# Four deals per tile, from one DMA queue or from two: the first layer of a graph network on one core

## The chip, the cores and the metric

The kernel runs on one core of a Trainium2 chip. The metric is the device time of one execution in microseconds (us); lower is better. Before the change it is 2586.3 us, the median of 3 runs (2586.27 to 2588.68).

## The reference

Four graph layers on x (2708 nodes x 512) with one adjacency matrix (2708 x 2708, zeros and ones, symmetric), all in f32. After each layer the result is added to x and layer-normalised. The change sits in layer 0:

```python
# layer 0: masked attention with 8 heads of 64
adj  = max(adj, eye)
q, k, v = x @ Wq[h], x @ Wk[h], x @ Wv[h]
att  = softmax(q @ k.T / 8 - 1e16 * (1 - adj))
out  = sum_h (att @ v) @ Wo[h]
x    = layernorm(x + out)
# layer 1: normalised adjacency times a two-step linear map
# layer 2: additive attention over the graph, leaky slope 0.2
# layer 3: normalised adjacency times x, linear map, relu
```

## The kernel before, in words

Layer 0 first projects x into KT (keys, transposed), V (values) and queries, which go to memory as `qtd` (lines 281 to 371; GpSimd issues those stores at line 348). Then it works through 84 full **pairs** and one last one: 21 chunks of 128 query rows (c) times 4 pairs of heads (p), and one remaining chunk of 20 rows.

For each pair the stages are these (class Pair, lines 399 to 528):

- `scores` (lines 426 to 448): TensorE multiplies queries by keys (line 417) into PSUM tiles of two heads; VectorE adds the mask, stores the scores in s and keeps their maxima (line 439). The 2708 columns are cut in two halves (k = 0 and 1) of 1408 and 1300, and each half in three parts.
- `maxima` (line 452), on VectorE, and `weights` (line 458), on ScalarE: exp of the scores, in place.
- The weights must then be turned, so that key nodes lie on the partitions. For the first 8 of the 128-column chunks of each half (16 of 22 chunks) this is done without TensorE: `blocks` (lines 460 to 467) transposes 32 x 32 blocks within the partitions on VectorE into a tile d (128 partitions x 2048 f32, 1 MB), and `deal` (lines 469 to 477) moves them across partitions by DMA into a tile e. d has four **node groups** of 32 partitions (g = 0 to 3); group g goes to `e[:, g]`, 32 source partitions with four runs of 2 KB each onto 128 destination partitions: 256 KB in one DMA, four DMAs for each tile, in the order g = 0, 2, 1, 3.
- `turn` (line 490) transposes the other 6 chunks on TensorE, and ScalarE copies them out of PSUM.
- `values` (lines 517 to 523): 44 products of V with the turned weights accumulate into av (line 509); ScalarE copies av to ot (line 527) and GpSimd issues the store of ot to `otd` in memory (line 528, 64 KB).

Tiles and buffers that matter: d has 2 buffers (line 385) and e has 3 (line 386). A pair uses one d and one e for each half. So a `blocks` may write its d only when the four deals out of the previous tile in this buffer have landed, and a deal may write its e only when TensorE has read the weights that lay there.

The order on TensorE, VectorE and ScalarE is written out by hand (manual_schedule, lines 609 to 651). One turn of that loop deals with three pairs: new (scores), cur (second half's blocks and deal, turn) and late (values). In each turn VectorE first writes the new pair's scores, then `cur.blocks(1)` (both heads, one instruction of 128 x 2048), then `new.blocks(0)` (one head at a time, two instructions of 128 x 1024), and the deals follow each:

```python
                if late is not None:
                    late.values()
                if cur is not None:
                    cur.blocks(1)
                    cur.deal(1)
                if new is not None:
                    for j in range(2):
                        new.blocks(0, slice(j, j + 1))
                    new.deal(0)
```

The queues of SyncE (SP) and GpSimd (POOL) are not under that manual schedule: the framework's scheduler places their instructions. On SP stand all eight deals of a turn and, once in four turns, the loads of the next chunk (queries, line 185, and three pieces of the adjacency rows, line 177). On POOL stands the store of ot, one for each pair. After layer 0 the other three layers follow with products, DMAs of adjacency tiles and small operations; the change does not touch them.

Of the kernel before, what the change touches and what calls it, by code (L numbers as in the profile page):

```python
# [22 lines left out]
def kernel(  # L23
# [22 lines left out]
    nc = tc.nc  # L46
# [99 lines left out]
    with ExitStack() as l0:  # L146
# [252 lines left out]
        class Pair:  # L399
# [69 lines left out]
            def deal(self, k):  # L469

                e = ep.tile([P, KD4, 2, DEALT, 32], F32, tag="e", name=f"e{self.c}_{self.p}_{k}")
                for g in (0, 2, 1, 3):
                    nc.sync.dma_start(
                        e[:, g].rearrange("p j m x -> p (j m x)"),
                        self.D[k][32 * g : 32 * g + 32].rearrange("p i j m x -> p i (j m x)"),
                    )
                self.E[bounds[k]] = e
# [908 lines left out]
```

## Time and profile before

| what | value |
|---|---|
| median of 3 runs | 2586.3 us |
| the profiled execution's own time | 2586.55 us |
| its span | 2584.8 us, so 1.75 us lie around it |
| mean granted TensorE clock | 0.989 |
| PE / DVE / ACT / POOL busy over the span | 97% / 76% / 45% / 12% |
| moved by SP's DMA queue (q1) | 392.0 MB, 53.4% of 16 engines' span |
| moved by POOL's DMA queue (q0) | 16.7 MB, 1.9% |
| pair loop of layer 0 | about 217 to 1228 us |
| DVE busy in 300 to 600, 600 to 900, 900 to 1200 us | 289.0, 291.5, 288.6 of 300 us each |
| ACT busy in the same | 224.7, 226.5, 223.1 of 300 us |
| DMA share in the same | 0.79, 0.79, 0.79 of 16 engines, 217 to 221 GB/s |

Rows of the profile name line, engine and operation, what is written and read, and how many; then busy time and mean duration, and the idle time that lay before them on their engine, with what ended most of it. The releaser after the arrow is inferred: of several waits it names the one that came last. SPq and POOLq are the queues of the DMA-issuing instructions: their durations are the time to issue, not to move the data. Durations of TensorE's matmuls are modelled, so a full PE is not by itself proof that PE is the limit.

### The profile page before, as it was taken

How to read it: one execution, taken by the hardware profiler on the slowest of the kernel's cores; microseconds unless marked ns; L12 is line 12 of the kernel's file. 1: busy time of each engine (PE TensorE's matmuls, PEld its weight loads, DVE VectorE, ACT ScalarE, POOL GpSimd, SP SyncE). 2: the span in 40 equal slices, each digit the busy share in tenths (PEclk: the TensorE clock that was granted, in tenths of full speed). 3: DMA queues.
4: the chain of work that ended last, by engine and by line, in shares of the span. 5: the costliest groups of instructions: out<-in, count | busy, mean ns of one | idle time of the engine just before them, and what ended most of it. 6: DMA issues, size and time to landing. Idle time of an engine off the chain costs nothing.

```text
span 2584.8 us, 42415 instructions
## 1 busy us (share of the span) xinstructions
PE 2514.1 (97%) x15551; PEld 1562.0 (60%) x15551; DVE 1959.6 (76%) x4541; ACT 1155.6 (45%) x2070; POOL 316.4 (12%) x322
## 2 busy tenths in 40 slices
PE   9999999999999999999899999899999999999997
PEld 4886777777777777776456444444444466444465
DVE  2669999999999999998474777888777874443544
ACT  2105777777777777776011001565665640000000
POOL 2210000000000000000210000243333430000000
PEclk9999999999999999999899999999999999999999
DMA  5115878778778787787753444344433213644633
GB/s 174 52 51 145 223 197 232 215 216 234 217 210 231 211 237 212 216 220 181 212 174 90 126 121 145 118 153 139 127 110 116 64 31 111 186 140 143 178 103 106
DMA packets 221498, 411.43 MB, mean 159 GB/s; under 512 B 28765, under 2 KB 48911, under 8 KB 221292
## 3 DMA queue, kind: packets, MB, share of 16 engines
q1 hardware_dynamic: 215052, 392.00, 53.4%
q0 software_dynamic: 6240, 16.73, 1.9%
q8 instruction: 123, 2.02, 0.3%
q14 instruction: 83, 0.68, 0.1%
HBM read 213.55 MB, written 16.72 MB: 89 GB/s over the span
## 4 chain that ended last, share of the span: by engine, by line
issue 49%; PE 40%; DVE 4%; POOL 3%; DMA 2%; ACT 1%; SPq 1%; POOLq 0%; ACTq 0%; DVEq 0%
PE acc L808 12%; PE acc L914 7%; PE m L1218 5%; PE pf L820 3%; PE psk L261 2%; POOL otd L528 2%; PE ph L900 1%; PE psq L261 1%; PE psv L261 1%; PE po L754 1%; PE p L945 1%; PE psv L357 1%; PE acc_t L808 1%; PE psq L309 1%; PE pz L820 1%
## 5 line engine op out<-in xcount | busy, mean ns | idle before, releaser
L458 ACT ACTIVATE s<-s,nm 128x1408 f32<-128x1408 f32 (+1 forms) x340 | 481.2, 1416 | 236.7 <-DVE nm L452 236.7
L439 DVE CUSTOM_DVE_ANT_0 s<-pss,adj 128x469 f32<-128x469 f32 (+2 forms) x1020 | 565.8, 622 | 1.1 <-PE pss L417 0.6
L417 PE MATMUL pss<-KT,qt 64*128 64x469 f32 (+2 forms) x2016 | 461.4, 559 | 7.0 <-DVE mx L439 4.8
L464 DVE STREAM_TRANSPOSE d<-s 128x1024 f32<-128x1024 f32 (+1 forms) x255 | 393.6, 1580 | 34.9 <-DMA e<-d 21.7
L417 PEld LDWEIGHTS pss<-KT,qt 64*128 64x128 f32 x2016 | 227.9, 186 | 200.0 <-issue 113.7
L808 PE MATMUL acc<-pt,x 128*128 128x512 f32 (+1 forms) x880 | 335.1, 540 | 12.7 <-ACT pt L861 9.7
L509 PE MATMUL av<-e,V 128*64 128x128 f32 x5376 | 308.8, 273 | 2.5 <-DMA e<-d 2.5
L509 PEld LDWEIGHTS av<-e,V 128*64 128x64 f32 x5376 | 296.8, 137 | 3.0 <-issue 3.0
L808 PEld LDWEIGHTS acc<-pt,x 128*128 128x128 f32 x880 | 158.8, 193 | 188.7 <-issue 164.4
L914 PE MATMUL acc<-at,h 128*128 128x512 f32 (+1 forms) x504 | 196.8, 543 | 0.0
L872 POOL TENSOR_TENSOR cs<-cs,pt 128x512 f32<-128x512 f32 (+2 forms) x110 | 157.4, 1431 | 203.2 <-ACT pt L861 200.1
L528 POOL DMA_DIRECT2D otd<-ot x84 | 45.4, 540 | 979.2 <-ACT ot L527 950.8
L859 DVE TENSOR_TENSOR pt<-pt,at 128x512 f32<-128x512 f32 (+2 forms) x132 | 107.4, 821 | 76.0 <-ACT pt L858 75.6
L1248 ACT ACTIVATE z<-pz,rdeg 128x512 f32<-128x512 f32 (+1 forms) x22 | 15.2, 689 | 310.4 <-PE pz L820 310.4
L94 ACT ACTIVATE ln_t<-lnve 128x1 f32<-128x1 f32 x88 | 17.7, 201 | 304.2 <-DVE lnve L108 304.0
L914 PEld LDWEIGHTS acc<-at,h 128*128 128x128 f32 x504 | 90.2, 190 | 101.4 <-issue 98.5
L490 PE MATMUL pst<-ident,s 128*128 128x128 f32 x1020 | 131.3, 279 | 0.0
L861 ACT ACTIVATE pt<-pt 128x512 f32<-128x512 f32 (+2 forms) x132 | 76.1, 579 | 109.4 <-DVE pt L860 109.2
L509 PEld LDWEIGHTS av<-pt,V 128*64 128x64 f32 x1680 | 90.0, 136 | 52.7 <-issue 52.5
L925 DVE SCALAR_TENSOR_TENSOR cs<-at,rdeg,cs 128x512 f32<-128x512 f32 (+2 forms) x126 | 86.2, 684 | 42.8 <-DMA at<-in_adjT_dram 41.8
L490 PEld LDWEIGHTS pst<-ident,s 128*128 128x128 f32 x1020 | 105.6, 134 | 17.3 <-issue 15.5
L509 PE MATMUL av<-pt,V 128*64 128x128 f32 x1680 | 110.3, 278 | 0.0
(348 smaller groups left out, 3484.5 us busy)
## 6 DMA issues: line engine op xcount, KB each, us to landing
e<-d SPq DMA_DIRECT2D x680, 256.0 KB
at<-in_adjT_dram SPq DMA_DIRECT2D x210, 256.0 KB
a<-in_adj_dram SPq DMA_DIRECT2D x38, 677.0 KB
adj<-in_adj_dram SPq DMA_DIRECT2D x42, 512.0 KB
at_a<-in_adjT_dram SPq DMA_DIRECT2D x40, 256.0 KB
at_c<-in_adjT_dram SPq DMA_DIRECT2D x40, 256.0 KB
at_f<-in_adjT_dram SPq DMA_DIRECT2D x40, 256.0 KB
adj<-in_adj_dram SPq DMA_DIRECT2D x21, 330.0 KB
```

The costliest lines, as they stand in the source:

```text
L261: nc.tensor.matmul(ps[:, p, :], ws[i][:, k, p * P : (p + 1) * P], xs[i][:, k, :], start=(k == 0), stop=(k == FC - 1),)
L417: nc.tensor.matmul(pss[j][:, :w], qt[h, self.p, :], KT[h, self.p, n0 : n0 + w], start=True, stop=True)
L439: nc.vector.tensor_tensor_reduce(out=s[:, j, h0:h1], in0=pss[j][:, : h1 - h0], in1=a[:, n0 + h0 : n0 + h1], scale=1.0, scalar=LOW, op0=ALU ...
L458: nc.scalar.activation(s, s, AF.Exp, bias=self.nm[:, j : j + 1], accum_out=self.sums(j, k))
L464: nc.vector.transpose(self.D[k].rearrange("p i j m x -> p j m i x")[:, heads], self.s[k][:, heads, : DEALT * P].rearrange("p j (m i x) -> ...
L490: nc.tensor.transpose(pt[:q, t, j, :], self.s[f][:, j, o : o + q], ident)
L509: nc.tensor.matmul(self.av[j * KD : (j + 1) * KD, out], V[:, m, h * KD : (h + 1) * KD], weights[j], start=(self.done == 0), stop=(self.don ...
L808: nc.tensor.matmul(acc[k][:, :w], last[0][g : g + mr, :] if m == NC - 1 else values[:mr, k * P : (k + 1) * P], moving[g : g + mr, :w], sta ...
L859: nc.vector.tensor_tensor(pt[:mr, :w], pt[:mr, :w], at[:mr, :w], ALU.subtract)
L872: nc.gpsimd.tensor_tensor(sums[:mr, :w], sums[:mr, :w], pt[:mr, :w], ALU.add)
L914: nc.tensor.matmul(acc[hc][:, :w], lastH[g : g + mr, :] if m == NC - 1 else H[m][:mr, hc * P : (hc + 1) * P], at[g : g + mr, :w], start=(m ...
L1218: nc.tensor.matmul(acc[k][:, : moving.shape[1]], combined[which, m][:, k * P : (k + 1) * P], moving, start=(m == 0), stop=(stop and m == N ...
```

## The change

In `deal`, the DMAs of node groups 2 and 3 are issued by GpSimd; those of groups 0 and 1 stay with SyncE. Size, shape, source and destination of every DMA are the same, and so is the order in which the code names them.

```diff
                 e = ep.tile([P, KD4, 2, DEALT, 32], F32, tag="e", name=f"e{self.c}_{self.p}_{k}")
                 for g in (0, 2, 1, 3):
-                    nc.sync.dma_start(
+                    (nc.gpsimd if g >= 2 else nc.sync).dma_start(
                         e[:, g].rearrange("p j m x -> p (j m x)"),
                         self.D[k][32 * g : 32 * g + 32].rearrange("p i j m x -> p i (j m x)"),
                     )
```

In the built program, 340 of the 680 deals stand on POOL's queue instead of SP's. POOL's order in a steady turn is: two deals of d(1), the first deal of d(0), the store of ot, the second deal of d(0). The waits of VectorE's transposes are as many as before (four DMA semaphores for each tile, two of them now POOL's); a deal now also waits on semaphores of the other queue's DMAs into the same e buffer. Layer 0's order on PE, DVE and ACT is unchanged; at the seam to layer 1 the scheduler exchanges a few dozen neighbouring instructions of PE, DVE and ACT (lines 85 to 111, 695 to 707, 755 and 900 to 925).

## The prediction, made before the changed kernel ran

> **What bounds the kernel.** I read the page's table of costliest groups first, then the busy time by stretch, then the transposes' and deals' own rows, then the timeline of one turn.
>
> ```profile
> L458 ACT ACTIVATE s<-s,nm 128x1408 f32<-128x1408 f32 (+1 forms) x340 | 481.2, 1416 | 236.7 <-DVE nm L452 236.7
> L439 DVE CUSTOM_DVE_ANT_0 s<-pss,adj 128x469 f32<-128x469 f32 (+2 forms) x1020 | 565.8, 622 | 1.1 <-PE pss L417 0.6
> L464 DVE STREAM_TRANSPOSE d<-s 128x1024 f32<-128x1024 f32 (+1 forms) x255 | 393.6, 1580 | 34.9 <-DMA e<-d 21.7
> ```
>
> These are all of ScalarE's exps and VectorE's two large groups in layer 0. ScalarE sits idle for VectorE (236.7 us). VectorE never waits for TensorE's scores (1.1 us in 1020), and nearly all its idle time there stands before L464, the block transposes, ended by a landing deal. The busy table says the same: in 600 to 900 us VectorE works 291.48 of 300 us. TensorE shows 300.00 of 300, but its ends are modelled: its weight loads wait 56.8 us in 203 places for VectorE's L439 to free a PSUM bank, so TensorE is the one with slack. **VectorE bounds the pair loop**, at 11.33 to 11.6 us for a pair without a stall (the spacing of its L452), with up to eight such pairs in a row.
>
> ```profile
> L473 SPq DMA_DIRECT2D e<-d x680: 542/920/2209, 221.7 to 1228.1; - x170
>   DMA e<-d: 21.7, 28
> ```
>
> The first row is the deals' issue time on SP (least, median, largest, in ns); the second comes from the list of what the transposes sat idle for: 28 waits of 0.78 us in the mean. The longest, 4.9 us, is at the last pair; 27 waits with 16.8 us lie between 250 and 1220 us. Where several semaphores end a wait only one is named: by the trace's completion records a deal lands just before the end of 28.3 us of such gaps, the 4.9 included, so 23.4 in the loop.
>
> One turn, from the timelines of DVE and SP:
>
> ```profile
> 712.22 2.31 DVE L464 STREAM_TRANSPOSE d<-s 128x2048 f32<-128x2048 f32 x1
> 714.70 1.25 DVE L464 STREAM_TRANSPOSE d<-s 128x1024 f32<-128x1024 f32 x1 [0.16 <-DMA e<-d]
> ```
> ```profile
> 703.02 7.49 SPq L473 DMA_DIRECT2D e<-d  x8
> ```
>
> The turn before, d(1) was ready at 702.96 and d(0) at 705.22. SP needs until 710.5 for its eight issues; the last begins at 709.90 and lands at 714.57, and the transpose that writes d(0) again could begin at 714.53. An ordinary turn has no slack for d(0); d(1) has 2.3 us (last landing 709.93, wanted 712.22). In turns with adjacency loads the landing is about 1 us later, and that is most of the 28 waits.
>
> **The change, part by part.**
>
> *SP's queue.* Four issues of each turn go. At the median of 920 ns eight are 7.4 us; the four that stay, at 0.54 to 0.92, are 2.2 to 3.7. SP can then start d(0)'s deals when d(0) is ready (705.2) instead of 706.7, 1.5 us sooner, and all loads behind them too. An issue takes 542 ns when nothing is in front of it and 0.6 to 1.35 us later in a burst: part of SP's time is back-pressure from transfers, so it isn't all won.
>
> *POOL's queue.* It gains four issues in a turn. The nearest row of the same size and shape (128 rows of 2 KB) is the output store, and the nearest in place is the store of ot, made in the midst of layer 0:
>
> ```profile
> L1252 POOL DMA_DIRECT2D out_dram<-y x22: 522/542/641, 2205.9 to 2576.5; - x22
> ```
> ```profile
> L528 POOL DMA_DIRECT2D otd<-ot x84: 540/540/557, 243.2 to 1226.2; - x84
> ```
>
> 4 x 0.54 + 0.54 = 2.7 us of an 11.6 us turn, on an engine busy 14 of 300 us: 340 x 0.54 = 184 us in all, wholly beside VectorE. If POOL issued like the store of queries (711 to 1036 ns, 512 short rows) it would be 4.7 us, still hidden. In the queue the store of ot stands before the last deal of d(0); its input is ready at 703.8 and that deal's at 705.2, so it holds nothing up. Without that cover the deal behind it would start late by the same amount. A deal waits on two or three more semaphores (earlier deals into its e buffer): TensorE has read that buffer, so they are past; the cost is queue time of some 20 to 60 ns each by the 17 to 50 ns of such instructions in the trace, off VectorE's path.
>
> *Whether POOL's issue is blocked.* The 84 stores take 540 to 557 ns while VectorE is 97% busy, so no price. The Trainium skill (SBUF — State Buffer, SBUF: two separate sides, "DVE blocks DMA") says that VectorE's two-port copies keep GpSimd from writing descriptors, 620 ns becoming 3100; as an estimate from that page four issues would take 12.4 us, over a turn, and the kernel would be bound by GpSimd. The row shows none of that beside these transposes and mask adds.
>
> *The transfers.* They decide. 2.1 MB a turn take from 704 to 713.6, 16 engines about 90% busy at 211 to 305 GB/s after a slow first 1.5 us at 78 to 86. If the engines are simply full, two queues end when one does. The trace has one microsecond in which both queues have work, at the end of the projections (start and end, then PE, PEld, DVE, ACT, POOL busy, clock, DMA share, GB/s):
>
> ```profile
> 200.00:201.00 1.00, 1.00 (x6) 0.89 (x5) 0.96 (x2) 0.36 (x1) 0.56 (x1) 1.00 0.98 266
> 201.00:202.00 1.00, 1.00 (x7) 0.87 (x6) 0.97 (x3) 0.00 (x0) 0.00 (x0) 1.00 0.85 197
> 202.00:203.00 1.00, 1.00 (x6) 0.90 (x5) 1.00 (x3) 0.00 (x0) 0.00 (x0) 1.00 1.00 381
> ```
>
> In the first two nearly all is POOL's queue (stores to memory); in the third 0.24 MB are SP's and 0.14 MB POOL's. One queue alone gets 197 to 266, both together 381. Bounds for a turn's 2.1 MB: at best 2.1/0.381 = 5.5 us against 9.6, 4 us sooner; at worst POOL's transfers are less efficient. If all ran at the 197 of POOL's poorest microsecond, 10.7 us, 1.1 later. I take 300 GB/s, between the 211 to 305 of the burst and the 381, nearer to the burst: 7.0 us, 2.6 sooner, less about 1 us because d(0) is ready only at 705.2 and POOL's transfers start late; some 1.5 us sooner is left. That covers all but the longest waits. The Trainium skill (DMA: Bandwidth & Descriptors, Issuing engines are not separate DMA queues) speaks against it: all run on the same 16 engines, several issuers save only the time to initiate. By that rule the landing, and the sum, would hardly move.
>
> *Sum.* Of 23.4 us in the loop I take 18, of the last pair's 4.9 us 2: **20 us**, from VectorE's path one for one, since runs of stall-free pairs show no other engine at 11.33 to 11.6 us. What is late next is VectorE itself. The seam's reordering: +-1 us, taken as 0. 2586.55 - 20 = **2566.5 us**. The profiled execution is 0.25 above the median, which I neglect.
>
> **Rivals.**
>
> *A. Same.* The 16 engines are the limit, not the issue. For: 90% busy in the burst, SP's issue drawn out to 920 ns. Against: the 381 GB/s. Burst ends as before: 2583 to 2590.
>
> *B. Slower.* POOL's half lands later than SP's did. A tile is free when its last quarter lands, and d(0) has no slack, so from the first 0.1 us every delay is paid in 84 turns. For: the store of ot, a quarter as large, takes 4.0 us to land, the same as a whole SP deal in a quiet queue (3.9 to 4.2); the queries' stores got only 197 to 266 GB/s. 0.5 us costs 84 x 0.5 = 42 us: 2628; the worst bound, 1.1 us, gives 2679. It decides once the burst's end is later than now.
>
> *C. Faster by little.* Only the short waits go (0.3 us gained): about 8 us, 2578. It is part of my forecast's range.
>
> **The numbers.** Forecast (with C) 0.62, its own range 2555 to 2580: the low end is all 31 us of idle before L464 but the loop's start. A 0.14, B 0.24. The range must leave out no more than 0.2: 2555 to 2620 leaves out the worse part of B (0.15) and little below. A measurement of this kernel tells 0.2% (5.2 us) from no change. Faster by more 0.61, within 0.15, slower 0.24.
>
> **What would show it.** Right: the wait of L464 for e<-d falls from 21.7 to under 5 us, SP's issues near 0.6 us, VectorE over 295 of 300 us, GB/s in the burst near 300. POOL's issues: 0.54 us each, 2.7 us a turn. Wrong if the idle time before L464 stays (A) or grows to an entry in every turn (B), or if TensorE waits for e. If POOL's issue takes over 1 us, the descriptor side is the cause, not the transfers.

## The result, and the profile after

| | before | after |
|---|---|---|
| median (lowest to highest) | 2586.28 us (2585.95 to 2588.68) | 2630.94 us (2628.74 to 2632.2) |
| profiled execution, its span | 2586.55, 2584.8 us | 2630.24, 2628.5 us |
| last deal of layer 0 issued at | 1228.1 us | 1277.0 us |

The change makes the kernel slower: ratio 1.016, 95% interval 1.0142 to 1.0177. (The two medians of the table alone give 1.0173. Against the median of all 52 times of the kernel before that are on record, 2589.13 us, it is 1.016.) The loss lies in the pair loop: its last deal is issued 48.9 us later. The span grows by 43.7, so what follows the loop is about 5 us shorter; why was not followed up.

The groups of VectorE and ScalarE in layer 0, after the change (busy time, mean ns | idle time before, and what ended it):

```profile
L458 ACT ACTIVATE s<-s,nm 128x1408 f32<-128x1408 f32 (+1 forms) x340 | 481.1, 1416 | 276.9 <-DVE nm L452 276.9
L439 DVE CUSTOM_DVE_ANT_0 s<-pss,adj 128x469 f32<-128x469 f32 (+2 forms) x1020 | 565.6, 621 | 3.3 <-PE pss L417 3.1
L464 DVE STREAM_TRANSPOSE d<-s 128x1024 f32<-128x1024 f32 (+1 forms) x255 | 395.3, 1583 | 76.9 <-DMA e<-d 54.4
```

Nothing became slower in itself: the busy times are those of before. What grew is the idle time before L464, from 34.9 to 76.9 us (+42.0), and ScalarE's wait for VectorE with it (+40.2). VectorE still bounds the loop; it now waits for deals. The deals' own rows say why it isn't the issue. These are the issues on either queue (least, median, largest ns; first and last start), then how long the transposes waited for a deal and how often, and the time from issue to landing:

```profile
L473 SPq DMA_DIRECT2D e<-d x340: 542/597/2732, 224.1 to 1274.5; - x170
L473 POOL DMA_DIRECT2D e<-d x340: 546/546/567, 224.7 to 1277.0; - x170
...
  DVE d L464: 54.4, 53
...
DMA to landing us min/median/max: 3.7/6.9/11.0
```

The median issue on SP fell from 920 to 597 ns, and GpSimd's is steady at 546. Yet 53 transposes instead of 28 end their wait with a landing, after 1.03 instead of 0.78 us. A landing 6.9 us after its issue isn't by itself late, because the issues of a turn now stand closer together; the completion records show that the burst ends later. Each DMA leaves up to 16 of them, one after another; what follows is worked out from the records, no view shows it. Counted from the end of the transposes that fill d(0), in the median of 64 turns in the middle of the loop:

| d(0) | before | after |
|---|---|---|
| first deal issued | 1.44 us | 0.07 us |
| last deal issued | 4.56 us | 1.62 us |
| last of the four deals landed | 9.05 us | 9.62 us |
| from a deal's first completion record to its last | 1.4 us | 3.4 us |

So the issues do come earlier, as they were meant to, and the tile is free 0.57 us later all the same: in 84 turns that is 48 us, about the loss. A deal's completions come further apart, and this holds for SP's deals as well as for GpSimd's. In 51 of the 64 turns SP's second deal, issued 0.66 us after d(0) was ready, is the last to land.

The busy table, before and after (start and end, then PE, PEld, DVE, ACT, POOL busy, clock, DMA share, GB/s):

```profile
300.00:600.00 300.00, 299.21 (x3146) 220.30 (x3144) 289.00 (x709) 224.73 (x389) 14.04 (x26) 1.00 0.79 221
600.00:900.00 300.00, 300.00 (x3147) 221.11 (x3145) 291.48 (x729) 226.49 (x390) 14.05 (x26) 1.00 0.79 219
900.00:1200.00 300.00, 299.74 (x3192) 222.00 (x3196) 288.63 (x720) 223.05 (x384) 13.50 (x25) 1.00 0.79 217
```
```profile
300.00:600.00 300.00, 297.96 (x3056) 215.80 (x3050) 278.58 (x688) 214.66 (x369) 65.02 (x120) 1.00 0.79 210
600.00:900.00 300.00, 297.24 (x3015) 214.55 (x3011) 280.70 (x694) 218.49 (x378) 68.27 (x126) 1.00 0.80 215
900.00:1200.00 300.00, 295.27 (x2975) 211.19 (x2974) 273.69 (x675) 213.18 (x366) 64.93 (x120) 0.99 0.77 205
```

The DMA engines are as busy as before (0.77 to 0.80 against 0.79), but move 205 to 215 GB/s instead of 217 to 221, and VectorE works 10 to 15 us less in each 300. So each byte costs more time of the DMA engines. The list of queues between 300 and 1190 us gives that for each queue (packets, MB, share of 16 engines' time), before:

```profile
q1 hardware_dynamic: 98655, 188.92, 76.7%
q0 software_dynamic: 2432, 4.97, 1.9%
```

and after:

```profile
q1 hardware_dynamic: 51811, 105.14, 40.0%
q0 software_dynamic: 25375, 80.28, 38.0%
```

Share x 16 x 890 us / MB is engine time for the bytes: 57.8 ns per KB on SP's queue before; 54.2 on SP's (q1) and 67.4 on GpSimd's (q0) after. Engine time isn't the same as lateness: SP's queue takes no more of it than before, and yet its deals land later.

### The profile page after: what moved, and what is told of

It reads as the page before. It is cut to its first block, busy times and chain, and to the rows that moved or that the text cites. A ratio compares the mean times of both kernels' runs of the same rounds, so it can differ in the third digit from the quotient of the medians.

```text
span 2628.5 us, 43054 instructions
## 1 busy us (share of the span) xinstructions
PE 2548.2 (97%) x15551; PEld 1572.3 (60%) x15551; DVE 1960.7 (75%) x4541; ACT 1156.1 (44%) x2070; POOL 500.6 (19%) x662
## 4 chain that ended last, share of the span: by engine, by line
PE 67%; issue 12%; DMA 10%; DVE 8%; ACT 2%; POOL 1%; SPq 0%; DVEq 0%; POOLq 0%; ACTq 0%
PE acc L808 13%; PE pss L417 12%; PE av L509 11%; DMA e<-d 8%; PE acc L914 7%; PE m L1218 4%; PE pst L490 3%; PE pf L820 3%; DVE d L464 2%; PE psk L261 2%; PE po L754 2%; PE ph L900 1%; PE psv L261 1%; PE psq L261 1%; PE p L945 1%
## 5 line engine op out<-in xcount | busy, mean ns | idle before, releaser
L417 PE MATMUL pss<-KT,qt 64*128 64x469 f32 (+2 forms) x2016 | 492.3, 568 | 14.9 <-DVE mx L439 11.1
L464 DVE STREAM_TRANSPOSE d<-s 128x1024 f32<-128x1024 f32 (+1 forms) x255 | 395.3, 1583 | 76.9 <-DMA e<-d 54.4
L417 PEld LDWEIGHTS pss<-KT,qt 64*128 64x128 f32 x2016 | 237.0, 187 | 229.1 <-issue 113.8
L473 POOL DMA_DIRECT2D e<-d x340 | 185.6, 548 | 830.2 <-PE pst L490 591.4
```

The costliest lines, as they stand in the source:

```text
L417: nc.tensor.matmul(pss[j][:, :w], qt[h, self.p, :], KT[h, self.p, n0 : n0 + w], start=True, stop=True)
L464: nc.vector.transpose(self.D[k].rearrange("p i j m x -> p j m i x")[:, heads], self.s[k][:, heads, : DEALT * P].rearrange("p j (m i x) -> ...
L473: (nc.gpsimd if g >= 2 else nc.sync).dma_start(e[:, g].rearrange("p j m x -> p (j m x)"), self.D[k][32 * g : 32 * g + 32].rearrange("p i j ...
```

## The experiments

Three theories. **T1:** GpSimd's side is the cause, its queue moves the deals less well than SP's. **T2:** two queues at once are. **T3:** it is from where the deals read: groups 0 and 1 are partitions 0 to 63, groups 2 and 3 are 64 to 127; the order 0, 2, 1, 3 alternates these halves, and the change gives each queue two deals out of one half in a row. All edits are in `deal`, that of experiment 3 in the loop too; ratios are to the kernel before on the same chip, with their 95% interval.

**1. All deals on GpSimd, in the old order.**

```diff
-                    nc.sync.dma_start(
+                    nc.gpsimd.dma_start(
```

> All four deals of a tile are issued by GpSimd, none by SyncE. Theory T1 (what GpSimd issues moves less efficiently, whatever runs beside it): all eight deals of a turn are now of the poor kind, slower than the split: 2640 to 2720 us, deals landing 7 us or more after their issue. Theory T2 (two queues feeding the same 16 engines delay each other's last quarter): the deals are in one queue again, only the store of ot and the loads are beside them: 2580 to 2595 us, landing near 4.6 us. Theory T3 (two deals in a row on one queue that read the same source side, groups 0 and 1 or 2 and 3, slow each other): the order 0, 2, 1, 3 is back within one queue, so about 2586 us.

2579.79 us, ratio 0.996 (0.9949 to 0.9972): a little faster than before, and the fastest version here that still computes the reference. The deals' issues and the transposes:

```profile
L473 POOL DMA_DIRECT2D e<-d x680: 546/548/583, 222.2 to 1230.5; - x170
```
```profile
L464 DVE STREAM_TRANSPOSE d<-s 128x1024 f32<-128x1024 f32 (+1 forms) x255 | 392.2, 1578 | 35.7 <-DMA e<-d 24.7 <-ACT s L458 4.4 <-ACT ot L527 2.2
```

The idle time is that of before, with twice as many deals on GpSimd as the change has. T1 falls. The last deal is issued at 1230.5 us, 2.4 later than before, while the span is 3.6 shorter: by these two profiles the gain isn't in the pair loop, and what makes it wasn't followed up.

**2. Groups 0 and 2 on SP, 1 and 3 on GpSimd.** Each queue now alternates the halves.

```diff
-                    nc.sync.dma_start(
+                    (nc.gpsimd if g in (1, 3) else nc.sync).dma_start(
```

> SyncE issues groups 0 and 2, GpSimd groups 1 and 3. T1: as the change, 2625 to 2640 us, since half the bytes are GpSimd's either way. T2: the same 2625 to 2640. T3: each queue alternates between the two halves of the partitions again, so most of the loss goes: 2575 to 2600 us.

2609.38 us, ratio 1.0075 (1.0052 to 1.0098): between before and the change, and outside all ranges expected. Which groups stand on which queue matters, but two queues still lose.

**3. The change's split with ScalarE in GpSimd's place** (its two deals of each tile follow the turn's copies).

```diff
+                    cur.deal(1, nc.scalar, (2, 3))
...
+                    new.deal(0, nc.scalar, (2, 3))
```

> Groups 0 and 1 by SyncE as in the change, groups 2 and 3 by ScalarE, behind the copies of turn, so that two queues are at work but GpSimd has no deal. ScalarE issues some 4 x 0.6 = 2.4 us a turn, which its 2.6 us of idle time a turn should just hold; its issues start 1 to 2 us later than GpSimd's did. T1: the transfers are as efficient as SyncE's: packets of 2 KB at 84 ns in most cases, a deal's first and last sixteenth landing about 1.5 us apart as before; time 2580 to 2605 us. T2: the sixteenths land 3 us apart as in the change, time 2620 to 2650 us. T3: the same as T2.

2714.24 us, ratio 1.0485 (1.0452 to 1.0517), and no answer:

```profile
L464 DVE STREAM_TRANSPOSE d<-s 128x1024 f32<-128x1024 f32 (+1 forms) x255 | 399.5, 1588 | 86.5 <-ACT s L458 71.4
```

The transposes now wait for ScalarE's exps, which stand behind ScalarE's issues in its order. That hides what the transfers do.

**4. All deals on SP, in the order 0, 1, 2, 3.** GpSimd has no part in it.

```diff
-                for g in (0, 2, 1, 3):
+                for g in (0, 1, 2, 3):
```

> All deals by SyncE, in the order 0, 1, 2, 3 instead of 0, 2, 1, 3. T1 and T2: 2584 to 2592 us, as before. T3: groups of one side in a row cost time: 2600 to 2640 us, with deals landing later than 4.7 us.

2635.15 us, ratio 1.0176 (1.015 to 1.0202): the loss of the change, without a second queue.

```profile
L464 DVE STREAM_TRANSPOSE d<-s 128x1024 f32<-128x1024 f32 (+1 forms) x255 | 395.3, 1583 | 75.5 <-DMA e<-d 49.9
```

75.5 us of idle time where the change has 76.9. Only the order of four equal DMAs is different from before. So the order of the sources is worth as much as the whole loss. But the change doesn't lose in quite the same way. By the completion records d(0)'s last deal lands 9.61 us after d(0) is ready, as late as after the change (9.62). Here it is issued at 4.74 us, later than before, and its completions stand 1.4 us apart as before; after the change it is issued at 1.62 us and they stand 3.4 apart.

**5 to 7. Other forms.** GpSimd alone in the order 0, 1, 2, 3; SP with 0, 2 and GpSimd with 3, 1, so that the queues should always read opposite halves; and whole tiles by queue, each in the old order.

```diff
-                for g in (0, 2, 1, 3):
-                    nc.sync.dma_start(
+                for g in (0, 1, 2, 3):          # pool_0123
+                    nc.gpsimd.dma_start(
...
+                for g in (0, 3, 2, 1):          # split_02_31
+                    (nc.gpsimd if g in (1, 3) else nc.sync).dma_start(
...
+                    (nc.gpsimd if k == 0 else nc.sync).dma_start(   # split_by_tile
```

> All deals by GpSimd, in the order 0, 1, 2, 3. T3: the loss of that order doesn't depend on the issuer: 2615 to 2645 us, against 2580 with GpSimd and the order 0, 2, 1, 3. If the loss belonged to SyncE's way of issuing alone: 2575 to 2590 us.

> SyncE issues groups 0 and 2, GpSimd 3 and 1: each queue alternates between the two halves of the partitions (0 to 63, 64 to 127), and the two queues stand on opposite halves at the same time. In the run with 0, 2 and 1, 3 they alternated but stood on the same half together. Theory T3 (what counts is the half that is read, over both queues together): the loss goes, 2575 to 2595 us. Theory T2 (two queues on the same engines delay each other's last quarter, on whatever half): as with 0, 2 and 1, 3, 2600 to 2620 us.

> The four deals of the second half's tile by SyncE, the four of the first half's by GpSimd, each in the order 0, 2, 1, 3: both queues have as many bytes as in the change and alternate halves, but each serves one tile, and GpSimd's start 2.3 us later in the turn. T3: near the kernel with one queue, 2575 to 2595 us. T2: 2600 to 2620 us, as GpSimd's four and SyncE's last two overlap.

GpSimd alone: 2644.78 us, 1.0208 (1.0181 to 1.0234), so the order costs on either queue. SP with 0, 2 and GpSimd with 3, 1: 2686.77, 1.0373 (1.0346 to 1.0399), the worst of the splits by group. By tile: 2692.02, 1.0399 (1.0366 to 1.0432). The last two lie above all ranges expected.

```profile
L464 DVE STREAM_TRANSPOSE d<-s 128x1024 f32<-128x1024 f32 (+1 forms) x255 | 395.9, 1583 | 135.7 <-DMA e<-d 91.9 <-ACT lastT L494 12.1 <-ACT s L458 11.5
```

This is split_02_31. For two queues T3 falls in the form that each queue must alternate the halves: here and by tile each does, and the loss is more than twice that of the change. The form over both queues together is not tested by it, for the queues didn't keep to opposite halves. By the completion records of d(1) (medians, from the time it is ready) group 3 on GpSimd completes from 4.0 to 7.4 us and group 2, of the same half, on SP from 4.5 to 9.0.

**8 and 9. Sources spread over all partitions,** deal g reading every fourth partition, with one queue and with the change's two. The weights then reach TensorE in another node order, so layer 0 no longer computes the reference; the DMAs' number, size and destinations stay.

```diff
-                        self.D[k][32 * g : 32 * g + 32].rearrange("p i j m x -> p i (j m x)"),
+                        self.D[k][g : P : 4].rearrange("p i j m x -> p i (j m x)"),
```

> All deals by SyncE in the order 0, 1, 2, 3, but deal g reads every fourth partition from g on (g, g+4, ...) instead of the 32 in a row; sizes and destinations stay, so the weights arrive in another order and layer 0 computes something else. Every deal now reads both halves of the partitions evenly. T3 (the source half is what the order is about): the 45 us that the order 0, 1, 2, 3 costs are gone, 2560 to 2592 us. If the order costs by something else than the source partitions: 2620 to 2645 us, as without the spreading.

> The change (0 and 1 by SyncE, 2 and 3 by GpSimd) with the same spread sources; layer 0 again computes something else. T3 alone (source halves are the whole loss): 2560 to 2592 us. T2 (two queues at work on the same engines cost by themselves): 2600 to 2640 us, although no deal prefers a half.

One queue, in the order 0, 1, 2, 3: 2550.61 us, 0.9863 (0.9846 to 0.9879). The change's split: 2547.58, 0.985 (0.9834 to 0.9866). Both are faster than every range expected. The split, its transposes and its busy table:

```profile
L464 DVE STREAM_TRANSPOSE d<-s 128x1024 f32<-128x1024 f32 (+1 forms) x255 | 388.1, 1572 | 7.9 <-DMA e<-d 2.1 <-ACT s L458 1.9 <-issue 1.1
```
```profile
300.00:600.00 300.00, 300.00 (x3244) 224.87 (x3242) 297.85 (x737) 232.23 (x401) 71.35 (x132) 1.00 0.65 227
600.00:900.00 300.00, 300.00 (x3235) 224.11 (x3233) 297.81 (x741) 232.93 (x402) 71.29 (x132) 1.00 0.65 228
```

The same queues, sizes, destinations and issues as in the change, and VectorE's idle time is gone (d(0)'s last deal lands after 6.32 us, not 9.62); more GB/s with a DMA share of 0.65 instead of 0.79. T2 in the form "two queues cost by themselves" falls: with these sources one queue and two give the same within their intervals.

**10. Half, or neighbourhood?** Every fourth partition changes two things: a deal reads from both halves, and no longer from 32 neighbouring partitions. In the next kernels deals 0 and 1 read the even and the odd partitions of 0 to 63, and 2 and 3 those of 64 to 127.

```diff
-                        self.D[k][32 * g : 32 * g + 32].rearrange("p i j m x -> p i (j m x)"),
+                        self.D[k][64 * (g // 2) + g % 2 : 64 * (g // 2) + 64 : 2].rearrange("p i j m x -> p i (j m x)"),
```

They run with SP alone in the order 0, 1, 2, 3 (half_0123), SP alone in 0, 2, 1, 3 (half_0213), and the split of the change (half_split).

> All deals on SyncE in the order 0,1,2,3, but deals 0 and 1 each read 32 partitions spread over one half of the source (the even and the odd ones of partitions 0 to 63), deals 2 and 3 the same of 64 to 127. Layer 0 computes something else (the weights arrive in another node order). It stands between the order 0,1,2,3 of 32 neighbouring partitions (2635) and that of every fourth partition (2551). If what counts is from which half of the partitions a queue reads in a row: 2615 to 2645, as the order 0,1,2,3. If what counts is that a deal reads 32 neighbours: at most 2592.

> All deals on SyncE in the order 0,2,1,3 of the kernel before, but deals 0 and 1 read the even and the odd partitions of 0 to 63, deals 2 and 3 those of 64 to 127 (layer 0 computes something else). The order alternates the halves as the kernel before does; only the 32 neighbours are gone. If half and neighbourhood are two costs that add: 2545 to 2565, as every fourth partition. If the alternation of halves already gives all that is to be had: 2580 to 2592. If the neighbourhood counts only within one half in a row: 2575 to 2592 too; the two are not told apart here.

> The same sources as in half_0213, with the split of the change: deals 0 and 1 (partitions 0 to 63) on SyncE, deals 2 and 3 (64 to 127) on GpSimd. Each queue reads from one half only, but both halves are open at any time. If each queue's own run on one half costs: 2595 to 2645. If only the sum over the queues counts, or only the neighbours: 2545 to 2570.

Together with the runs above (ratio, and the difference at 2586.3 us):

| a deal's 32 source partitions | SP, 0, 2, 1, 3 | SP, 0, 1, 2, 3 | split of the change |
|---|---|---|---|
| neighbours | 1 (before) | 1.0176, +46 us | 1.016, +41 us |
| even or odd ones of one half | 0.9933, -17 us | 1.0036, +9 us | 0.9915, -22 us |
| every fourth of all | not run | 0.9863, -35 us | 0.985, -39 us |

Intervals of the middle row: 0.9913 to 0.9952, 1.0025 to 1.0048, 0.9884 to 0.9945. The medians are 2571.08, 2598.67 and 2568.16 us. half_0123 met neither of its two expectations: it lies between them, so the half and the neighbourhood both count. half_0213 met none of its three; half_split met its second. Read down the last column: in half_split each queue still reads from one half only, yet it is as fast as half_0213. So **a queue's run on one half is not enough for the change's loss; it needs deals that read 32 neighbouring partitions**. By the completion records d(0)'s last deal lands after 8.47 us in half_split and a deal's completions stand 1.4 us apart, with issues at the same times as in the change (the last at 1.60 us). Its transposes, and the list of queues between 300 and 1190 us:

```profile
L464 DVE STREAM_TRANSPOSE d<-s 128x1024 f32<-128x1024 f32 (+1 forms) x255 | 390.5, 1575 | 24.7 <-DMA e<-d 14.6 <-ACT s L458 3.6 <-ACT pt L496 1.8
```
```profile
q1 hardware_dynamic: 55523, 110.06, 43.1%
q0 software_dynamic: 26784, 84.74, 34.8%
```

55.8 ns per KB on SP's queue, about as after the change (54.2); 58.5 on GpSimd's, instead of 67.4. So the extra engine time is that of GpSimd's transfers, and of these only with 32 neighbours and SP's deals beside them: alone in the old order (experiment 1) its queue took 56.0.

With one queue, read along the rows: the run on one half costs 46 us with neighbours and 27 with even and odd ones.

**11. All on SP in the order 0, 2, 3, 1,** so that the first two deals of a tile alternate, but pairs of one half follow each other.

```diff
-                for g in (0, 2, 1, 3):
+                for g in (0, 2, 3, 1):
```

> All deals on SyncE, in the order 0,2,3,1: between tiles and within a tile there are now runs of two deals out of one half of the partitions (2,3 and 1,0), as in 0,1,2,3, but the first two of a tile alternate. If runs of two on one half cost: 2610 to 2640. If only the first two deals of a tile matter: 2580 to 2595.

2612.45 us, ratio 1.0087 (1.0072 to 1.0102): runs of two on one half cost on one queue, about half of what 0, 1, 2, 3 does.

**12. Finer deals on GpSimd:** eight of 16 partitions for each tile, halves alternating; then the same with every eighth partition as source.

```diff
-                for g in (0, 2, 1, 3):
-                    nc.sync.dma_start(
-                        e[:, g].rearrange("p j m x -> p (j m x)"),
-                        self.D[k][32 * g : 32 * g + 32].rearrange("p i j m x -> p i (j m x)"),
-                    )
+                for g0, h in ((0, 0), (0, 1), (1, 0), (1, 1)):
+                    for g in (g0, g0 + 2):
+                        nc.gpsimd.dma_start(
+                            e[64 * h : 64 * h + 64, g].rearrange("p j m x -> p (j m x)"),
+                            self.D[k][32 * g + 16 * h : 32 * g + 16 * h + 16].rearrange("p i j m x -> p i (j m x)"),
+                        )
...
+                            self.D[k][2 * g + h : P : 8].rearrange("p i j m x -> p i (j m x)"),   # fine_spread
```

> All deals by GpSimd, each cut in two of 16 source partitions (128 KB), in the order 0, 2, 0, 2, 1, 3, 1, 3: the halves alternate twice as often, at twice the issues (16 x 0.55 = 8.8 us a turn, beside 11.6). T3: deals conflict less, 2565 to 2580 us against 2580. If the issue then is the limit (the last deal of d(0) issued at about 705.2 + 8 x 0.55 + the rest of d(1)'s, 711, where it was 709): 2590 to 2620 us.

> All on GpSimd, eight deals of 128 KB for each tile as in pool_fine, which took 2738, but each reads every eighth partition of all 128; the destinations are the same 64 neighbouring partitions (layer 0 computes something else). If the sources made pool_fine slow: 2550 to 2620. If its twice as many deals or their destinations on 64 neighbours did: 2690 to 2740.

2737.71 us, ratio 1.0576 (1.0552 to 1.06), and with spread sources 2702.87, 1.0433 (1.0406 to 1.0461). pool_fine lies above both its ranges, fine_spread in the upper of its two. So the sources make about 35 us of it, and the rest is the number of deals or their destinations, 64 neighbouring partitions. The number alone would do. The deals of fine_spread:

```profile
L474 POOL DMA_DIRECT2D e<-d x1360: 500/540/622, 221.7 to 1333.2; - x195
```

16 a turn at 540 ns are 8.6 us. By the completion records d(0)'s last deal is issued 6.1 us after d(0) is ready (4.6 before the change) and lands after 10.4 (9.05 before): 1.3 us later, in 84 turns 112 us, which is what the ratio gives. That is read from the records; the destinations were not tried by themselves.

## Why the prediction was wrong

The forecast was 2566.5 us with a range of 2555 to 2620; 2630.94 lies outside, on the other side.

- **What bounds the loop:** right. VectorE, idle almost only before L464, and a deal's delay is paid about one for one: the idle time before L464 grew by 42.0 us, the loop's last issue came 48.9 later, and the span grew by 43.7.
- **SP's queue:** right. "SP's issues near 0.6 us" was forecast; the median is 597 ns. d(0)'s first deal was to start 1.5 us sooner; it did by 1.4 (from 1.44 to 0.07 us after d(0) is ready).
- **GpSimd's queue:** right. 0.54 us each, beside VectorE; measured 546, at most 567 ns. The Trainium skill's trap (SBUF — State Buffer, SBUF: two separate sides, "DVE blocks DMA") does not show here, as the stores' row had said.
- **The transfers:** this step failed. "I take 300 GB/s ... some 1.5 us sooner is left." Measured were 205 to 215 GB/s in the loop, less than the 217 to 221 of before, and d(0)'s last deal landed 0.57 us later instead of 1.5 sooner. The number came from one microsecond at the end of the projections, in which SP's queue loaded and GpSimd's stored. I read its 381 GB/s as what two queues give. Experiments 8 to 10 show that with spread or half sources one queue or two makes no difference clear of the noise, and that the source partitions decide: with the same two queues the time is 2547.6, 2568.2 or 2630.9 us. A rate from transfers with other sources says little of these. It was also not the one microsecond in which both queues have work, as I wrote: the store of ot runs beside SP's deals. In the turn that I read, 706 to 707 us moved 336 GB/s, by these queues (packets, MB, share):

  ```profile
  q1 hardware_dynamic: 163, 0.28, 80.4%
  q0 software_dynamic: 23, 0.05, 17.1%
  ```

  And "one queue alone gets 197 to 266" holds of GpSimd's stores only; the burst's own 305, which I give for it, is SP's queue almost alone.
- **Rival B** was right in that a tile is free when its last quarter lands and that every turn pays for it, and its price was near: 0.5 us in 84 turns, 2628 us. I gave it 0.24. It had the wrong half late: SP's second deal is mostly the last of d(0), not GpSimd's. Its "for" was the store of ot's slow landing, thus GpSimd's queue as such; experiment 1 shows that the queue as such is not slower. The reason to look for stood in the code: four DMAs of equal size in the order 0, 2, 1, 3 instead of 0, 1, 2, 3. I priced the number of issues that moved and not the order that they broke up; experiment 4 shows that this order alone is worth 46 us on one queue.
- The rule that I weighed against the change (the Trainium skill, DMA: Bandwidth & Descriptors, Issuing engines are not separate DMA queues) says that several issuers only save time to initiate. Spread sources agree with it: 2550.6 us from one queue, 2547.6 from two. With 32 neighbours SP and GpSimd together are slower than one queue in the old order by 0.75 to 4%, of which it says nothing.
- A section of the Trainium skill that I didn't weigh bears on the rest (SBUF — State Buffer, Door 1: The DMA port swizzle): partitions 0 to 63 reach the same 8 of 16 DMA ports as 0 to 31 do, 64 to 127 the other 8. The runs agree in part: a run on one half costs 27 or 46 us on one queue, and every fourth partition beats the best half by 17 or 18 us. They don't agree where even and odd partitions of a half should do no better than 32 neighbours, which reach the same ports: the split gains 63 us by it. There the measurement decides.

**What stays open:** why the completions of deals of 32 neighbours come so far apart when two queues work, why only GpSimd's queue shows more engine time, and why 0, 2 against 3, 1 is the worst pairing by group. The trace doesn't say which DMA engine moved a packet. A version that computes the reference with spread sources was not run: a deal would have to read four node groups and write four slots of e in one DMA.

## What to carry to other kernels

Before DMAs are split over queues, write down for each queue which source and destination partitions follow each other before and after; an order such as 0, 2, 1, 3 may be worth more than the issue time that is saved. (The destinations were never varied by themselves here.) Don't borrow a bandwidth from another stage unless its transfers read and write the same partitions: here that error made a loss look like a gain of 20 us. To learn whether a queue or the data's place is the cause, run the same order on one queue, and the same queues with other sources: two kernels of a changed line or two each settled here what the views of the profile could not.

## What the runs showed of the hardware that I had not expected

- The order of four equal 256 KB DMAs on one queue is worth 1.76% of the whole kernel, and spreading their sources gains 1.4% on the kernel before, at a DMA share of 0.64 instead of 0.79 (in a kernel that then computes something else).
- GpSimd issues such a DMA in 546 to 583 ns even with 680 of them beside a VectorE that is 95 to 98% busy. SP's issues of the same DMAs stretch to 2209 ns in the kernel before, and with all deals on GpSimd the kernel is 0.4% faster (0.9949 to 0.9972).
- The two queues cut the same DMA differently: between 300 and 1190 us SP's queue before has 79332 packets of 2048 bytes, GpSimd's after 19583 of 4096. (The lists' means, 1.9 KB for 188.92 MB in 98655 packets and 3.2 KB for 80.28 MB in 25375, count packets of 4 bytes too.)
